# A sandwich layer on one core: the last row's addition on TensorE, the very last row centred ahead of its scale, two blocks re-timed, the FFN's small tensors loaded later

## The chip, the cores and the metric

The kernel runs on 1 core of one Trainium2 chip. The metric is device time in microseconds of one execution; the median of several runs counts. A core has five engines that run their own instruction streams: TensorE (matmuls, into PSUM), VectorE, ScalarE, Pool (GpSimd) and SyncE, which here only issues transfers. They wait for one another by semaphores.

## The reference

The input is 1024 rows of 512 values, in float32. Everything is float32.

```python
x = x + layernorm(attention(layernorm(x)))       # 32 query heads, 8 key/value heads, head size 128, causal
x = x + layernorm(ffn(layernorm(x)))

def attention(x):
    q, k, v = x @ w_q, x @ w_k, x @ w_v          # (512, 4096), (512, 1024), (512, 1024)
    probs = softmax(causal(q k^T * 128 ** -0.5))
    return (probs v) @ w_o                       # (4096, 512)

def ffn(x):
    base_out = x @ base_W.T + base_b             # 512 to 512
    probs = softmax(x @ router_W.T + router_b)   # 15 logits
    w = sum over the 8 largest probs, by expert_map[index]
    h = x @ A.T                                  # 8 experts of rank 16
    return base_out + 2.0 * ((h * w) @ B)

layernorm(x) = (x - mean) / sqrt(var + 1e-5)
```

## The kernel before, in words

**Blocks.** One block is a pair (g, t): a key/value group g of 8 (it has four query heads) and a tile t of 128 rows, of 8. There are 64 blocks. Blocks 0 to 47 (`i < N2`) are groups 0 to 5 in order, each with t = 0 to 7, so that block i is (i//8, i%8); the last 16 interleave groups 6 and 7, two tiles at a time. "Third block" is t=2, "fourth" t=3. Odd groups are g = 1, 3, 5. The rows 512 wide of the eight tiles are gathered in `acc[t]`.

**Inside a block.** The 128 rows are taken in four steps (`NSUB`), each 32 rows of all four heads. `scores(g, t, j)` makes one step's scores on TensorE into a PSUM buffer of two (`s`, two rows of the trace for each 512 columns, since a float32 matmul shows as two). VectorE adds the mask (L691) and takes the maximum (L693), ScalarE the exponential (L698, which frees the PSUM buffer), VectorE the reciprocal (L708), ScalarE the scaling (L709), VectorE a 32x32 transposition into `T` (L715). Pool clears the part of `p` above the diagonal ahead of each step (L672). After the fourth step sixteen transfers bring `T` into `K` (`to_keys`, tile names `K<-T`), on SyncE's queue, or a third of them on Pool's queue in blocks t = 1, 2, 3 of odd groups. Two blocks later `weighted_values` multiplies `K` with the values (`po`, 512 columns, t+1 terms), ScalarE copies the result (L746, `attnT`), and two row tiles at a time `project_o_pair` multiplies with `w_o` (`pa` to `pe`, seven products in 256 columns instead of eight, with sums of operands on VectorE, L796 to L799, and additions into `acc`, L820).

**What fills TensorE.** Between the four score matmuls of block i the main loop hands out other TensorE work, `then`: query, key and value projections for later blocks (`pq`, `pk`, `pv`, also in seven products, in pieces of 128 columns), `po` of block i-2 and, for even i, `pa` to `pe` of the pair before. Each piece has a price in columns, and `run_share` gives step n the pieces whose middle lies between `shares[n]` and `shares[n + 1]` of the total. `weave` merges two lists by price. TensorE keeps the program's order; so do most instructions of the other engines (`keep`, `order`), and the others are placed by a scheduler's estimates.

```python
        if i % 2 and i // 2 + 1 in QW and blocks[i][1] > 1 and 3 < i < N2:
            cut = len(rest) * 3 // 5
            q, rest = weave(q, rest[:cut]), rest[cut:]
```

In an odd-numbered block `rest` is `po`'s terms: two for t=3 (those of block t=1), four for t=5, six for t=7.

**Pool's queue.** Weight and input sums of the seven-product scheme run there (L189: `tx`, `sq`, `sk`, `sv`, `wot`). Right after block 8, (1,0), `prepare_ffn` issues six transfers on Pool's queue for tensors which the FFN needs in the last group (`ra_sb` in two parts, `bt_sb`, `bias_bc`, `rb_bc`, `emap_i`; 256 KB each for three of them). After block 12, (1,4), `prepare_map` builds `mexp` from `emap_i` on VectorE in nine small instructions (L330, L333).

**The end.** When the last score has been taken, an order written out by hand finishes four row tiles c, d, e, f. Row e goes through `ffn_out`: bias (L940), statistics (L344 to L348), reciprocal square root as a power on Pool (L350), shift (L359), normalization on ScalarE (L360), addition into `acc` by VectorE (L944), store. The very last, f, goes through `ffn_out_last`: the same in halves (L976, L977), statistics (L981, L983), power on Pool (L985), then on VectorE centring and scaling in one instruction (L987) and the addition (L988), and its store. The four stores stand in SyncE's queue in the order c, d, e, f. Row e's addition stands in VectorE's queue between f's L983 and L987.

Of the kernel before, what the change touches and what calls it, by code (L numbers as in the profile page):

```python
# [12 lines left out]
ALU = mybir.AluOpType  # L13
# [9 lines left out]
def kernel(  # L23
# [33 lines left out]
    nc = tc.nc  # L57
# [4 lines left out]
    NT = S // P  # L62
# [27 lines left out]
    blocks = [(g, 2 * u + e) for g, u in pairs for e in range(2)]  # L90
    N = len(blocks)
    N2 = (G - 2) * NT
# [5 lines left out]
    def keep(ins):  # L98
        return tc.keep_in_program_order(ins)
# [5 lines left out]
    def matmul(*args, **kw):  # L105
        keep(nc.tensor.matmul(*args, **kw))  # L106
# [181 lines left out]
    ident = const.tile([P, P], F32, tag="ident", name="ident")  # L288
# [77 lines left out]
    def bank(name):  # L366
        return ps_m.tile([P, 512], F32, tag="pm", name=name)
# [271 lines left out]
    def defer(t, *steps, first=False):  # L639

        if held:
            held[t].extend(steps)
            return
        deferred[:0] = steps if first else ()
        deferred.extend(() if first else steps)
# [194 lines left out]
    state = {}  # L840
# [75 lines left out]
    def ffn_out(t):  # L916

        pf = []

        def base(k):  # L920
            if k == 0:

                if t in (c, e):
                    pf.append(ps_s.tile([P, S], F32, tag="s", name=f"pf_{t}")[:, :512])
                else:
                    pf.append(bank(f"pf_{t}"))
            matmul(pf[0], state["hT", t][:, k, :], weights["base", k], start=(k == 0), stop=False)

        def turn_hw():
            pt = bank(f"ptw_{t}")  # L930
            transpose(pt[:, :ER], state.pop(("hw", t)).rearrange("p e r -> p (e r)"), ident)
            hwT = state["hwT", t] = ffn.tile([ER, P], F32, tag="hwT", name=f"hwT_{t}")
            copy = nc.scalar.copy(hwT, pt[:, :P])
            if held:
                keep(copy)

        def finish():
            matmul(pf[0], state.pop(("hwT", t)), bt_sb, start=False, stop=True)
            y = ffn.tile([P, H], F32, tag="hy", name=f"y_{t}", bufs=3)
            order(nc.vector.tensor_tensor(y, pf[0], bias_bc, ALU.add))  # L940
            statistics, norm = layernorm(y, y, f"y{t}", nc.scalar)

            def add_y(by=nc.gpsimd):
                order(by.tensor_tensor(acc[t], y, acc[t], ALU.add))  # L944
                state["done", t] = True

            if held and t == e:
                defer(t, statistics, norm, lambda: add_y(nc.vector))
            else:
                defer(t, statistics, lambda: (norm(), add_y()))  # L950

        w = [(512, lambda k=k: base(k)) for k in range(KC)]
        return w[:2], [(P, turn_hw)], w[2:], [(512, finish)]

    def ffn_out_last(t):


        halves = [slice(n * hn, (n + 1) * hn) for n in range(2)]
        pf = {}

        def base(n, k):
            if k == 0 and n == 0:
                pf[n] = ps_s.tile([P, S], F32, tag="s", name=f"pf_{t}_{n}")[:, :hn]
            elif k == 0:
                pf[n] = bank(f"pf_{t}_{n}")[:, :hn]
            w = weights["base", k][:, halves[n]]
            matmul(pf[n], state["hT", t][:, k, :], w, start=(k == 0), stop=False)

        def finish(*between):

            hwT = state.pop(("hwT", t))
            y = ffn.tile([P, H], F32, tag="hy", name=f"y_{t}", bufs=3)
            stats = small.tile([P, 2, 6], F32, tag="stats2", name=f"stats_y{t}", bufs=1)
            for n in range(2):
                matmul(pf[n], hwT, bt_sb[:, halves[n]], start=False, stop=True)
                keep(nc.vector.tensor_tensor(y[:, halves[n]], pf[n], bias_bc[:, halves[n]], ALU.add))  # L976
                keep(nc.vector.bn_stats(stats[:, n, :], y[:, halves[n]]))  # L977
                if n == 0:
                    between[0]()
            mv = small.tile([P, 2], F32, tag="mv", name=f"mv_y{t}")  # L980
            keep(nc.vector.bn_aggr(mv, stats))  # L981
            ve = small.tile([P, 1], F32, tag="ve", name=f"ve_y{t}")
            keep(nc.vector.tensor_scalar(ve, mv[:, 1:2], EPS, None, ALU.add))  # L983
            rstd = small.tile([P, 1], F32, tag="rstd", name=f"rstd_y{t}")
            keep(nc.gpsimd.tensor_tensor(rstd, ve, neg_half, ALU.pow))  # L985
            between[1]()
            keep(nc.vector.tensor_scalar(y, y, mv[:, 0:1], rstd, ALU.subtract, ALU.mult))  # L987
            keep(nc.vector.tensor_tensor(acc[t], y, acc[t], ALU.add))  # L988
            state["done", t] = True

        return [[(hn, lambda n=n, k=k: base(n, k)) for k in range(KC)] for n in range(2)], finish
# [7 lines left out]
    c, d, e, f = (blocks[k][1] for k in (N - 6, N - 5, N - 2, N - 1))  # L999
# [134 lines left out]
    for i in range(N):  # L1134
        loads(i)
        q, other = projections(i)
        pv = attend(i - 2) if i >= 2 else []
        o, o_pair, ends, begins = [], [], [], []
        for t in complete(i, 3):
            o = project_o(*blocks[i - 3])  # L1140
        if i % 2 == 0 and i >= 4 and blocks[i - 4][0] < G - 1:
            if i == 4:
                rescale_scores()
            o_pair = project_o_pair(*pairs[i // 2 - 2])
        for t in complete(i, 6, 7):
            ends = sum(ffn_out(t), [])
        for t in complete(i, 5):
            begins = ffn_router(t)

        rest = o + weave(o_pair, other + pv[:2] + begins[1:] + pv[2:])  # L1150
        if i in (N2, N2 + NT // 2):
            rest = weave(o_pair, pv) + other
        if i == N2 + 1:
            rest = pv[:3] + other + pv[3:]

        if i % 2 and i // 2 + 1 in QW and blocks[i][1] > 1 and 3 < i < N2:
            cut = len(rest) * 3 // 5
            q, rest = weave(q, rest[:cut]), rest[cut:]
        then = begins[:1] + q + ends[:-1] + rest[:4] + ends[-1:] + rest[4:]
        if i % 2 and i // 2 + 1 in QL:  # L1160
            cut = max(4, len(rest) - 4)
            then = begins[:1] + ends[:-1] + rest[:4] + ends[-1:] + rest[4:cut] + q + rest[cut:]
        shares = [n / NSUB for n in range(NSUB + 1)]
        if o_pair and blocks[i][0] % 2 == 0 and blocks[i][1] == 2 and i < N2:

            shares[3] = 0.8
        for n in range(NSUB):
            scores(*blocks[i], n)
            run_share(then, shares[n], shares[n + 1])
            m = i // 2 + 1  # L1170
            if i % 2 == 0 and m in QL and n == 2:
                todo.extend(last_sums(m))
            if i >= N2 + NT and i // 2 + 1 in QL:
                for dst, p, q, op in [todo.pop(0) for _ in range(min(LATE[i % 2, n], len(todo)))]:
                    keep(nc.gpsimd.tensor_tensor(dst, p, q, op))
            if i % 2 == 0 and m in QW and m not in QL:
                if n == 0 and i < N2:
                    combine_x(pairs[m][1], m)
                if n == (1 if i < N2 else 0):
                    combine_q(m)  # L1180
            g, t = blocks[i]
            if g % 2 and g + 1 < G and n == 1:
                if t == 6:
                    combine_k(g + 1)
                if t == 7:
                    combine_v((g + 1) // GV)
            if (i, n) in ((N2, 3), (N2 + 1, 2), (N2 + 2, 2)):
                combine_x(i - N2 + 1, 0)

            alone = i < 2 or i >= N2 or blocks[i][1] == NT - 1  # L1190
            pool_off(len(pool_jobs) if alone else -(-len(pool_jobs) // (NSUB - n)))
        if i == 2:
            combine_o(0)
        if i == NT:
            prepare_ffn()
        if i == NT + 4:
            prepare_map()
        for t in complete(i, 2):
            reload_x(t)
        ready += complete(i, 7, 8)  # L1200
        for t in [t for t in ready if ("done", t) in state]:
            ready.remove(t)
            ffn_store(t)

        if i >= NT and blocks[i - 2][1] == 0 and blocks[i - 2][0] < G - 1:
            combine_o(blocks[i - 2][0])
            if i >= N2:
                pool_off(len(pool_jobs))
# [79 lines left out]
```

## Time and profile before

| | |
|---|---|
| median of 3 runs | 1056.83 us (1056.42 to 1057.2) |
| profiled execution | 1056.89 us, of which span 1055.1 us |
| TensorE clock granted | 0.998 |
| TensorE busy | 1041.9 us (99%) |
| VectorE, ScalarE, Pool busy | 756.4, 477.0, 286.5 us |
| last TensorE matmul ends, last store is issued | 1046.4, 1050.5 us |

Times in the text are microseconds from the span's start unless they are durations. In the trace's timeline a line has start, duration, engine, line of the kernel, operation, output<-inputs, how many were merged (x4), and in brackets the idle time of the engine ahead of it and what ended it. Matmuls overlap their successors, so their start times tell more than their durations. In the waits a line reads: who, waited for whom: microseconds in total, times, longest. PE is TensorE, DVE VectorE, ACT ScalarE, POOL Pool, SP SyncE; a q behind the name is the engine's sequencer.

### The profile page before, as it was taken

What the parts mean: (1) busy time and instruction counts of PE and PEld (TensorE: products, weight loads), DVE (VectorE), ACT (ScalarE), POOL (GpSimd) and SP (SyncE); (2) the same over time, 40 slices, a digit from 0 to 9 for tenths busy, and PEclk for the clock granted to TensorE, in tenths of its full rate; (3) what the DMA queues carried; (4) which work ended last, traced back from release to release, by engine and by line L of the source; (5) the groups of instructions that cost most, each with busy time, mean ns of one, the idle gap of its engine ahead of it and who ended that gap; (6) DMA issues with size and microseconds to landing.
All of it is one profiled execution on the core that took longest, in us unless ns stands there. A gap on an engine that the chain in (4) does not pass through costs nothing.

```text
span 1055.1 us, 15845 instructions
## 1 busy us (share of the span) xinstructions
PE 1041.9 (99%) x4936; PEld 733.1 (69%) x4936; DVE 756.4 (72%) x1849; ACT 477.0 (45%) x961; POOL 286.5 (27%) x522
## 2 busy tenths in 40 slices
PE   9999999999999999999999999999999999999996
PEld 7766667767787676767787667767788565666553
DVE  4576657876587766887477875886667967687766
ACT  3655434554244544553244543654234654454421
POOL 2513025241030213341031312542162112333112
PEclk9999999999999999999999999999999999999999
DMA  5145352563126352453324443464333673543331
GB/s 189 36 125 137 74 122 70 136 158 83 40 53 163 90 121 68 117 145 81 81 51 120 110 105 72 127 168 120 85 106 91 150 190 90 148 113 95 85 91 40
DMA packets 78515, 112.01 MB, mean 106 GB/s; under 512 B 18176, under 2 KB 49920, under 8 KB 78432
## 3 DMA queue, kind: packets, MB, share of 16 engines
q1 hardware_dynamic: 75248, 106.24, 40.0%
q0 software_dynamic: 2096, 3.46, 1.4%
q10 hardware_dynamic: 1088, 1.31, 0.4%
q8 instruction: 40, 0.66, 0.3%
q14 instruction: 43, 0.35, 0.1%
HBM read 33.34 MB, written 2.10 MB: 34 GB/s over the span
## 4 chain that ended last, share of the span: by engine, by line
PE 91%; DVE 3%; SPq 2%; ACT 1%; DMA 1%; issue 1%; POOL 0%; POOLq 0%; DVEq 0%; ACTq 0%
PE po L106 22%; PE s L106 21%; PE pq L106 18%; PE pv L106 5%; PE pk L106 5%; PE pe L106 4%; PE pa L106 4%; PE pf L106 3%; PE pO L106 2%; PE pc L106 2%; PE pb L106 2%; PE pd L106 2%; SPq L112 2%; DMA K<-T 1%; DVE T L715 1%
## 5 line engine op out<-in xcount | busy, mean ns | idle before, releaser
L709 ACT ACTIVATE p<-p,rec 128x32 f32<-128x32 f32 (+31 forms) x256 | 188.1, 735 | 239.5 <-DVE rec L708 183.9
L106 PE MATMUL po<-K,v 128*128 128x512 f32 x576 | 280.7, 594 | 1.1 <-DMA K<-T 0.8
L106 PE MATMUL s<-kT,qT 128*128 128x512 f32 (+15 forms) x768 | 272.5, 464 | 0.8 <-ACT p L698 0.7
L698 ACT ACTIVATE p<-s,nmax 128x32 f32<-128x32 f32 (+31 forms) x256 | 179.5, 701 | 164.7 <-DVE nmax L693 148.3
L715 DVE STREAM_TRANSPOSE T<-p 128x128 f32<-128x128 f32 (+7 forms) x256 | 197.6, 773 | 52.5 <-ACT p L709 41.0
L106 PEld LDWEIGHTS s<-kT,qT 128*128 128x128 f32 x768 | 140.1, 190 | 116.3 <-issue 103.3
L693 DVE TENSOR_REDUCE nmax<-s 128x1 f32<-128x32 f32 (+31 forms) x256 | 180.1, 704 | 7.2
L672 POOL MEMSET p<- 128x96 f32 (+2 forms) x192 | 29.1, 152 | 544.3 <-DVE T L715 494.7
L106 PEld LDWEIGHTS po<-K,v 128*128 128x128 f32 x576 | 103.1, 190 | 58.8 <-issue 49.5
L513 DVE TENSOR_TENSOR qT<-pq,qT 128x256 f32<-128x256 f32 x174 | 77.8, 461 | 38.0 <-ACT qT L539 20.8
L691 DVE TENSOR_TENSOR s<-s,smask 128x32 f32<-128x32 f32 x256 | 47.9, 187 | 76.4 <-PE s L106 75.5
L106 PEld LDWEIGHTS pq<-xnT,wq 128*128 128x128 f32 x560 | 75.4, 191 | 9.5 <-issue 6.6
L106 PE MATMUL pq<-xnT,wq 128*128 128x128 f32 (+1 forms) x560 | 81.6, 293 | 0.0
L746 ACT COPY attnT<-po 128x512 f32<-128x512 f32 x64 | 37.4, 584 | 71.9 <-PE po L106 71.6
L106 PE MATMUL pa<-wo,attnT 128*128 128x256 f32 x224 | 58.5, 385 | 0.0
L106 PEld LDWEIGHTS pq<-tx,wq 128*128 128x128 f32 x416 | 53.0, 192 | 7.9 <-issue 7.5
L106 PE MATMUL pq<-tx,sq 128*128 128x128 f32 x416 | 57.5, 275 | 0.0
L106 PEld LDWEIGHTS pq<-tx,sq 128*128 128x128 f32 x416 | 53.4, 192 | 5.7 <-issue 5.0
L106 PE MATMUL pq<-tx,wq 128*128 128x128 f32 x416 | 55.4, 275 | 0.0
L106 PEld LDWEIGHTS pa<-wo,attnT 128*128 128x128 f32 x224 | 41.1, 190 | 14.1 <-issue 9.3
L708 DVE RECIPROCAL rec<-total 128x1 f32<-128x1 f32 x256 | 39.2, 153 | 16.2 <-ACT p L698 15.1
L698 ACT ACTIVATION_READ_ACCUMULATOR p<-s,nmax 128x1 f32 x256 | 49.6, 194 | 0.0
(164 smaller groups left out, 1327.9 us busy)
## 6 DMA issues: line engine op xcount, KB each, us to landing
K<-T SPq DMA_DIRECT2D x128, 128.0 KB, 2.4
K<-T SPq DMA_DIRECT2D x128, 112.0 KB, 2.3
wq<-in_w_q_dram SPq DMA_DIRECT2D x27, 512.0 KB, 5.1
K<-T SPq DMA_DIRECT2D x128, 96.0 KB, 2.2
K<-T SPq DMA_DIRECT2D x128, 80.0 KB, 2.1
wo<-in_w_o_dram SPq DMA_DIRECT2D x32, 256.0 KB, 3.5
K<-T SPq DMA_DIRECT2D x108, 64.0 KB, 2.0
K<-T SPq DMA_DIRECT2D x113, 48.0 KB, 1.9
```

The costliest lines, as they stand in the source:

```text
L106: keep(nc.tensor.matmul(*args, **kw))
L112: keep(by.dma_start(dst, src))
L513: nc.vector.tensor_tensor(dst, src, to, ALU.add)
L672: keep(nc.gpsimd.memset(p[:, t * P + (j + 1) * SQ : (t + 1) * P], 0.0))
L691: keep(nc.vector.tensor_tensor(s[:, n - SQ : n], s[:, n - SQ : n], smask, ALU.add))
L693: keep(nc.vector.tensor_reduce(nmax, s[:, :n], AX.X, ALU.max, negate=True))
L698: keep(nc.scalar.activation(p[:, :n], s[:, :n], AF.Exp, bias=nmax, accum_out=total))
L708: keep(nc.vector.reciprocal(rec, total))
L709: keep(nc.scalar.mul(p[:, :n], p[:, :n], rec))
L715: nc.vector.transpose(turned[g, t][:, :, j, :, :].rearrange("p b k q -> p k b q"), p[:, :full].rearrange("p (k b q) -> p k b q", b=R, q=SQ),)
L746: copy = nc.scalar.copy(o, po)
```

## The change

- Row e's last addition: instead of VectorE adding, TensorE multiplies `acc[e]` and then y by the identity into one PSUM bank, and ScalarE copies the bank into `acc[e]`.
- Row f: VectorE first subtracts the mean (one instruction that needs no power), then multiplies with the power and adds in one instruction.
- t=3 of groups 1 to 5: of `po`'s two terms none is woven into the query pieces (before: one); for t=5 and 7 as before.
- t=2 of odd groups: the fourth score matmul comes after 0.8 of the other work instead of 0.75, as it did already in even groups.
- `prepare_ffn` after block 12 instead of 8, `prepare_map` after block 16 instead of 12.

```diff
+            def add_on_pe():
+                pm = bank(f"padd_{t}")
+                matmul(pm, ident, acc[t], start=True, stop=False)
+                matmul(pm, ident, y, start=False, stop=True)
+                keep(nc.scalar.copy(acc[t], pm))
+                state["done", t] = True
+
             if held and t == e:
-                defer(t, statistics, norm, lambda: add_y(nc.vector))
+                defer(t, statistics, norm, add_on_pe)
...
-            keep(nc.vector.tensor_scalar(y, y, mv[:, 0:1], rstd, ALU.subtract, ALU.mult))
-            keep(nc.vector.tensor_tensor(acc[t], y, acc[t], ALU.add))
+            keep(nc.vector.tensor_scalar(y, y, mv[:, 0:1], None, ALU.subtract))
+            keep(nc.vector.scalar_tensor_tensor(acc[t], y, rstd, acc[t], ALU.mult, ALU.add))
...
-            cut = len(rest) * 3 // 5
+            cut = len(rest) * (4 if blocks[i][1] == 3 else 6) // 10
...
-        if o_pair and blocks[i][0] % 2 == 0 and blocks[i][1] == 2 and i < N2:
+        if o_pair and blocks[i][1] == 2 and i < N2:
             shares[3] = 0.8
...
-        if i == NT:
+        if i == NT + 4:
             prepare_ffn()
-        if i == NT + 4:
+        if i == NT + 8:
             prepare_map()
```

## The prediction, before the change was run

> **What bounds the kernel now.** I read the page first: TensorE is busy nearly all the time and carries the chain.
>
> ```profile
> PE 1041.9 (99%) x4936; PEld 733.1 (69%) x4936; DVE 756.4 (72%) x1849; ACT 477.0 (45%) x961; POOL 286.5 (27%) x522
> PE 91%; DVE 3%; SPq 2%; ACT 1%; DMA 1%; issue 1%; POOL 0%; POOLq 0%; DVEq 0%; ACTq 0%
> ```
>
> So an edit pays only where it closes a hole in TensorE's row or shortens the end after its last matmul. The page's matmul ends are modelled, so I measured holes by start times. Two 256-column rows start 0.216 us apart (eight in 1.73 us), two of 224 columns 0.189 apart; a start later than that is a hole. The waits of TensorE name the two that this diff can reach:
>
> ```profile
> PE po L106 <- DMA K<-T: 0.8, 1, 0.8
> PE s L106 <- ACT p L698: 0.7, 2, 0.3
> ```
>
> The first, in TensorE's timeline, and on the chain that ended last:
>
> ```profile
> 148.88 0.54 PE L106 MATMUL s<-kT,qT 128*128 128x224 f32 x2
> 150.19 2.38 PE L106 MATMUL po<-K,v 128*128 128x512 f32 x5 [0.76 <-DMA K<-T]
> ...
> 141.82 6.69 DMA K<-T
> 148.53 1.61 DMA K<-T
> ```
>
> `po` of block (0,7) was due at 148.88+2x0.189=149.26 and began at 150.19: 0.93 late. It waited for a transfer that took 6.69 us. The DMA view of 134 to 152 us shows what it met, and the page shows its usual time, 2.4:
>
> ```profile
> K<-T SPq DMA_DIRECT2D x16, 128.0 KB, 3.0
> ra_sb<-in_a_t_dram POOLq DMA_DIRECT2D x1, 256.0 KB, 5.0
> bt_sb<-in_b_t_dram POOLq DMA_DIRECT2D x1, 256.0 KB, 5.5
> bias_bc<-in_base_b_dram POOLq DMA_DIRECT2D x1, 256.0 KB, 6.6
> ...
> K<-T SPq DMA_DIRECT2D x128, 128.0 KB, 2.4
> ```
>
> The second, in group 3's third block (TensorE, then ScalarE), with the same place in group 2, where the share is 0.8 already:
>
> ```profile
> 411.19 1.03 PE L106 MATMUL pd<-wo,sums 128*128 128x256 f32 x4
> 412.55 0.91 PE L106 MATMUL s<-kT,qT 128*128 128x384 f32 x2 [0.33 <-ACT p L698]
> 412.29 0.20 ACT L698 ACTIVATION_READ_ACCUMULATOR p<-s,nmax 128x1 f32 x1
> ...
> 289.46 0.59 PE L106 MATMUL pe<-wo,sums 128*128 128x256 f32 x2
> 289.95 0.91 PE L106 MATMUL s<-kT,qT 128*128 128x384 f32 x2
> ```
>
> Due at 411.19+0.86=412.05, it began at 412.55, when ScalarE had freed the score buffer. In group 2 two rows of `pe` fill that time and the start is 0.06 late.
>
> Last, the end:
>
> ```profile
> 1048.07 0.68 DVE L944 TENSOR_TENSOR acc<-y,acc 128x512 f32<-128x512 f32 x1
> 1048.30 0.86 POOL L985 TENSOR_TENSOR rstd_y<-ve_y,neg_half 128x1 f32<-128x1 f32 x1 [1.69 <-DVE ve_y L983]
> 1049.19 0.55 DVE L987 TENSOR_SCALAR y<-y,mv_y,rstd_y 128x512 f32<-128x512 f32 x1 [0.44 <-POOL rstd_y L985]
> 1049.77 0.69 DVE L988 TENSOR_TENSOR acc<-y,acc 128x512 f32<-128x512 f32 x1
> L1284 POOLq DRAIN  x3: 46/102/5961, 1048.3 to 1054.7; - x3
> ```
>
> The last store is issued at 1050.50 and lands at 1052.50; SyncE has checked its semaphores by 1053.07. But Pool's own drain, queued behind the power, runs 5.96 us from 1048.27 to 1054.23, and the closing barrier comes after it. Stores have 1.16 us to spare.
>
> **FFN's small tensors later.** `prepare_ffn` issues six Pool DMAs (139.10 to 142.79, 3.69 us of Pool); they go from behind block 8 to behind block 12, Pool's `tx` sums there ending at 192.69, so about 192.7 to 196.4. Without them the sixteen K transfers of block 7, the last issued at 143.89, land in about 2.4 us, near 146.3, three before `po` is due. The hole goes: 0.93, and 0.07 by which the first row after it ran slow. **-1.00 us.** At the new place: block 11's K transfers end at 194.19, 2.7 before their reader; on Pool the six pass only `p`'s memset of 194.25, now about 196.4, whose exponential begins at 201.43; `wo` (four of 256 KB, issued 192.87 to 194.84) isn't read before its sums on Pool at 294.1. Then come block 12's K transfers, issued from 197.78, landed 210.21, read at 210.92: 0.71 us of cover, the thinnest. I take nothing there, because they ask for 80 KB each 0.63 us against block 7's 128 KB, and the DMA share was 0.56 (192 to 211) against 0.82 (134 to 150); the other end is a rival. `prepare_map` goes from block 12 to block 16: 0.17+0.70 us of VectorE leave the spot just before the transpose that releases block 12's K (so it may start up to 0.87 sooner) and come behind an addition that ends at 261.92 after 1.63 us of idleness; cover: TensorE has projections there. Nothing.
>
> **Share 0.8 in odd groups' third block.** Two rows of `pe` (0.43 us) move in front of the fourth scores. In groups 3 and 5 (holes at 411.8 and 656.3, both 0.50 and 0.10 of slow restart) the hole becomes group 2's 0.06 and 0.10: 2x0.43, **-0.86 us.** Group 1 has no hole at 166.93; its scores come 0.43 later, against 3.0 us of cover of that block's K. In groups 3 and 5 the scores keep their absolute time while TensorE's later work comes 0.43 sooner, and VectorE may put `acc<-pe` (0.69) before their maximum, so the block's K loses 0.4 to 1.1 us of cover: 2.4 in group 3, 1.0 in group 5. Zero to 0.1.
>
> **Fourth block.** The diff says odd groups, but the condition holds for t=3 of groups 1 to 5. The first of two `po` terms moves behind the query pieces. Four pieces of 128 columns stand for one of 512, so each score matmul keeps its distance in TensorE's work; the last `po` stays where it was, and VectorE's sums wait for that one. No hole over 0.07 us lies in these blocks. Nothing; bounds 0.4 either way, a hole of the size seen elsewhere (0.44 at 326.4).
>
> **The end.** Row e: its addition leaves VectorE (0.68 us). The first 512-column pair runs in TensorE's idleness after 1046.4; the second waits for ScalarE's y (done 1047.84) and ends at 1047.90+0.43+0.59=1048.92; the copy, priced by L380's 0.59, ends near 1049.6. So row e's store goes from 1048.78 to about 1049.64 and holds SyncE until 1050.0. Row f: centring (0.55 by L987) starts at 1048.07 and ends at 1048.62. It isn't free beside the power: Pool's power takes 0.55 where VectorE reads PSUM (1029.46), but here it ended 0.41 behind L944's end. Centring being 0.13 shorter than L944, the power ends near 1049.03. The fused multiply-add has no row; 0.55 (one input) to 1.38 (two passes of L988) bound it, and I take L988's 0.69 for its two tensor inputs: 1049.76, store at 1050.02 behind row e's. If the drain counts from the power's end, as I take it, the span ends **0.13 us** sooner; if it counts from its own start, nothing. If instead stores set the end, row f's packets queue behind row e's (0.8 us each, by packets of the last two): 1049.64+2.0+0.8=1052.4, 0.06 sooner; without that queueing 0.47. The Trainium skill, "SBUF — State Buffer", section "SBUF: two separate sides", says that the port pair shared by VectorE and GpSimd is an exclusive lock, and that the blocked side starts about 0.115 us after VectorE's end. By it the title's "while Pool takes its power" is no overlap; the rows agree (0.86 against 0.55). With a true overlap the power would end at 1048.85 and the sum would be 0.18 better.
>
> **Sum:** 1.00+0.86+0.13=1.99. The profiled execution took 1056.89 (span 1055.1 and 1.8 around it), against a median of 1056.83: 1054.90 from the one, 1054.84 from the other. **Forecast 1054.8 us.** What a measurement of this kernel can tell from no change is about 0.2%, 2.1 us, so the forecast lies on that line.
>
> **Rivals.** *More than summed:* the hole at 326.4 (0.44, K of group 2's fourth block, landing 3.57 us after its issue) closes with the re-timed block, and the end gains 0.47 because stores bind: 1.00+0.86+0.44+0.47=2.77, 1054.1. For it: Pool's other two drains took 0.10 and 0.05, so the long one may wait for something outside Pool; against: nothing in the t=3 edit moves that block's last transpose. The Trainium skill, "VectorE: DVE Perf Modes", section "The DRAIN you can't avoid", gives boilerplate drains about 12 ns, by which the stores would bind; the 5961 ns above speaks against it here.
>
> *The re-timing is handed back:* group 5's third block runs out of its 1.0 us, or group 3's scores wait for the later exponential in block four (I count 0.4 us of cover). Then 0.86 returns: 1055.7. Against it: even groups live with 0.8, though their fourth block is longer.
>
> *The collision moves (slower):* the six loads meet `wo` and block 12's K. Block 7's last transfer landed in 6.1 us; at that price instead of 2.1, less 0.71, TensorE waits 3.3 us at 210.9: 1056.83-1.99+3.3=1058.1. It decides for slower when that landing takes over 2.1+0.71+1.99=4.8 us. Against: spare DMA time before the last is issued at 208.09.
>
> **Chances.** Forecast 0.62 (own range 1054.1 to 1055.4; about 0.34 of it beyond 0.2%), more 0.18, handed back 0.10, collision 0.10 (half of it over 0.2%). Faster 0.34+0.18=0.52; same 0.28+0.10+0.05=0.43; slower 0.05. The range 1053.8 to 1056.2 holds the first three and leaves out the collision and the outer edges.
>
> **What would show it.** Right: no TensorE wait on `K<-T` near 149, no 0.33 us waits on `p` L698, K transfers near 141 landing in 2.4 us, block 12's `po` unbroken near 209, power 0.7 to 0.8 us. Wrong: a new TensorE wait on `K<-T` near 210 or in group 5's fifth block, waits on `p` in a fourth block, or an end more than 0.3 us off its old distance from the last `pf` matmul.

## The result

The changed kernel took 1054.93 us (median of 21 runs, 1054.42 to 1055.62) against 1056.77 for the kernel before beside it (21 runs, 1055.92 to 1057.3): ratio 0.9983, 95% interval 0.9976 to 0.9989. That is 1.84 us less. The profiled execution took 1054.94 with a span of 1053.2, clock 0.999. The forecast was 1054.8.

The page after, and TensorE's longest waits:

```profile
PE 1043.6 (99%) x4940; PEld 733.7 (70%) x4940; DVE 755.5 (72%) x1848; ACT 477.1 (45%) x962; POOL 285.8 (27%) x522
```
```profile
PE idle L109 <- POOL ident masks.py:199: 1.5, 1, 1.5
PE padd L106 <- ACT y L360: 0.7, 1, 0.7
PE pc L106 <- DVE acc L818: 0.7, 1, 0.7
PE po L106 <- DMA K<-T: 0.3, 1, 0.3
```

The two waits of before are gone from this list (`s` for `p` L698) or another one (the `po` that still waits for `K<-T` is at 995.3, not at 149). TensorE's timeline at the two places:

```profile
148.99 0.54 PE L106 MATMUL s<-kT,qT 128*128 128x224 f32 x2
149.37 1.88 PE L106 MATMUL po<-K,v 128*128 128x512 f32 x4
...
410.72 0.59 PE L106 MATMUL pe<-wo,sums 128*128 128x256 f32 x2
411.22 0.91 PE L106 MATMUL s<-kT,qT 128*128 128x384 f32 x2
```

`po` follows the scores at their 2x0.189 us, and two rows of `pe` stand where the 0.50 us of waiting stood. The DMA view of 134 to 152 us has the sixteen K transfers with nothing beside them:

```profile
K<-T SPq DMA_DIRECT2D x16, 128.0 KB, 2.4
K<-T SPq DMA_DIRECT2D x11, 16.0 KB, 1.9
```

The end, from the timeline and from the rows of the closing barrier (its line is L1293 now):

```profile
1046.42 0.48 DVE L996 TENSOR_SCALAR y<-y,mv_y 128x512 f32<-128x512 f32 x1
1046.65 0.65 POOL L993 TENSOR_TENSOR rstd_y<-ve_y,neg_half 128x1 f32<-128x1 f32 x1 [1.69 <-DVE ve_y L991]
1047.34 0.75 DVE L997 SCALAR_TENSOR_TENSOR acc<-y,rstd_y,acc 128x512 f32<-128x512 f32 x1 [0.44 <-POOL rstd_y L993]
1047.40 0.59 ACT L952 COPY acc<-padd 128x512 f32<-128x512 f32 x1 [1.22 <-PE padd L106]
```
```profile
L1293 POOLq DRAIN  x3: 46/102/5751, 1046.6 to 1052.9; - x3
L1293 SPq DRAIN  x3: 7/7/7, 1051.2 to 1052.6; - x3
```

Pool's long drain shrank from 5961 to 5751 ns, as the power in front of it shrank from 0.86 to 0.65 us.

The following table gives TensorE's holes (late start and slow restart together, us) at the places that matter, for the traces of the experiments too. The last row is from the first `pv` matmul to the last group of `pf`, which leaves out the first 8 us and the end.

| near us | before | before again | FFN alone | share alone | cut alone | end alone | share + cut | after | after, no cut |
|---|---|---|---|---|---|---|---|---|---|
| 55 | 0.38 | 0.16 | 0.28 | 0.08 | 0.08 | 0.42 | 0.16 | 0.44 | 0.08 |
| 149 | 1.00 | 1.36 | 0 | 0.84 | 0.94 | 0.91 | 0.83 | 0 | 0 |
| 326 | 0.44 | 0 | 0.42 | 0 | 0 | 0 | 0 | 0 | 0 |
| 412 | 0.60 | 0.60 | 0.60 | 0.17 | 0.60 | 0.60 | 0.17 | 0.17 | 0.17 |
| 424 | 0 | 0 | 0 | 0.64 | 0 | 0 | 0 | 0 | 0.64 |
| 656 | 0.60 | 0.60 | 0.60 | 0.17 | 0.60 | 0.60 | 0.17 | 0.17 | 0.17 |
| 670 | 0 | 0 | 0 | 0.64 | 0 | 0 | 0 | 0 | 0.64 |
| 698 | 0 | 0 | 0 | 0 | 0 | 0 | 0.08 | 0.20 | 0 |
| 995 | 0.16 | 0.15 | 0.15 | 0.46 | 0.15 | 1.23 | 0.31 | 0.50 | 0.45 |
| 1011 | 0.84 | 0.87 | 0.86 | 0.51 | 0.86 | 0.29 | 1.06 | 0.85 | 0.51 |
| first `pv` to last `pf` | 1037.27 | 1036.90 | 1036.15 | 1036.77 | 1036.42 | 1037.22 | 1036.05 | 1035.56 | 1035.86 |

Between the first traces of before and after, four holes close by 1.00+0.44+0.43+0.43=2.30 and others open by 0.34+0.20+0.06=0.60 (near 995, 698 and 55). The row of distances gives 1.71. The hole near 995 is 0.31 to 0.66 in all eight traces of kernels with the share and 0.14 to 0.16 in five of the six without it (the sixth, 1.23, is told further down), so some 0.3 us of it goes with the share; why stays open.

### The profile page after: what moved, and what is told of

It reads as the page before. It is cut to its first block, busy times and chain, and to the rows that moved or that the text cites. A ratio compares the mean times of both kernels' runs of the same rounds, so it can differ in the third digit from the quotient of the medians.

```text
span 1053.2 us, 15841 instructions
## 1 busy us (share of the span) xinstructions
PE 1043.6 (99%) x4940; PEld 733.7 (70%) x4940; DVE 755.5 (72%) x1848; ACT 477.1 (45%) x962; POOL 285.8 (27%) x522
## 3 DMA queue, kind: packets, MB, share of 16 engines
q10 hardware_dynamic: 1088, 1.31, 0.4%
## 4 chain that ended last, share of the span: by engine, by line
PE 94%; DVE 3%; SPq 1%; issue 1%; ACT 1%; POOL 0%; DMA 0%; POOLq 0%; DVEq 0%; ACTq 0%
PE po L106 22%; PE s L106 21%; PE pq L106 19%; PE pv L106 5%; PE pk L106 5%; PE pe L106 5%; PE pa L106 4%; PE pf L106 3%; PE pO L106 2%; PE pc L106 2%; PE pd L106 2%; PE pb L106 2%; SPq L112 1%; PE pl L106 1%; PE idle L109 1%
## 5 line engine op out<-in xcount | busy, mean ns | idle before, releaser
L698 ACT ACTIVATE p<-s,nmax 128x32 f32<-128x32 f32 (+31 forms) x256 | 179.5, 701 | 161.1 <-DVE nmax L693 141.8
L513 DVE TENSOR_TENSOR qT<-pq,qT 128x256 f32<-128x256 f32 x174 | 77.4, 459 | 35.7 <-ACT qT L539 19.1
L698 ACT ACTIVATION_READ_ACCUMULATOR p<-s,nmax 128x1 f32 x256 | 49.6, 194 | 0.0
```

Of the source, the lines that this page charges most:

```text
L513: nc.vector.tensor_tensor(dst, src, to, ALU.add)
L698: keep(nc.scalar.activation(p[:, :n], s[:, :n], AF.Exp, bias=nmax, accum_out=total))
```

## The experiments

**The four parts, each alone on the kernel before.** Medians of 11 executions each, against 1056.62. None of the four intervals excludes 1, so what a part does is read from its trace and not from its time.

*FFN's small tensors:*

```diff
-        if i == NT:
+        if i == NT + 4:
             prepare_ffn()
-        if i == NT + 4:
+        if i == NT + 8:
             prepare_map()
```

> Only the FFN's small tensors are moved (the six Pool DMAs four blocks later, and the expert map's two VectorE steps four blocks later). My theory: the hole before block (0,7)'s po goes (0.92 + 0.08 us in the trace of before), and nothing takes its place, so the last group of pf matmuls starts 1.0 us sooner and the time is 1055.8 against 1056.8 of before. Rival 'collision moves': block 12's po waits for K and the gain is below 0.5. Second question: the hole of 0.44 us at 326.4, gone in the changed kernel, for which nothing in my steps accounts. If it goes here too, more is gained, 1.4 us (1055.4), and it belongs neither to the share nor to the fourth blocks.

1055.76 us, ratio 0.9993 (0.9984 to 1.0001): 0.86 less. The hole at 149 is gone, block 7's K last landed at 146.30, and block 12's K landed 1.14 us ahead of its reader, so no collision. The hole at 326 is here (0.42), so this edit does not close it.

*The share:*

```diff
-        if o_pair and blocks[i][0] % 2 == 0 and blocks[i][1] == 2 and i < N2:
+        if o_pair and blocks[i][1] == 2 and i < N2:
             shares[3] = 0.8
```

> Only the share of 0.8 for the third blocks of odd groups. My theory: the holes at 411.8 and 656.3 shrink from 0.50 to 0.07 us each, 0.86 in all: 1055.9 us against 1056.8, with the hole near 149 unchanged. Rival 'handed back': a new wait of TensorE in the fourth or fifth block of group 3 or 5 takes some of it, and the gain is under 0.5. If the hole that the changed kernel has at 697.8 (0.20 us, group 5's fifth block) is here too, it is the price of this edit; if not, it has another cause.

1056.83 us, ratio 1.0002 (0.9993 to 1.0011): no gain. The holes at 412 and 656 shrink by 0.43 each, as forecast; two new ones of 0.64 stand at 424 and 670. (The texts on record give the second as 0.56: there another hole of 0.08, which stands beside it in every kernel, was taken off.) TensorE's waits of this kernel name them, and the timelines of VectorE and TensorE show why:

```profile
PE s L106 <- DVE qT L513: 0.8, 2, 0.4
```
```profile
423.20 0.20 DVE L691 TENSOR_TENSOR s<-s,smask 128x32 f32<-128x32 f32 x1 [0.26 <-PE s L106]
423.77 0.71 DVE L715 STREAM_TRANSPOSE T<-p 128x512 f32<-128x512 f32 x1 [0.38 <-ACT p L709]
424.41 0.65 DVE L693 TENSOR_REDUCE nmax<-s 128x1 f32<-128x512 f32 x1
424.98 0.74 DVE L513 TENSOR_TENSOR qT<-pq,qT 128x256 f32<-128x256 f32 x2
```
```profile
423.22 1.06 PE L106 MATMUL pq<-tx,sq 128*128 128x128 f32 x8
424.11 1.02 PE L106 MATMUL po<-K,v 128*128 128x512 f32 x2
425.54 1.24 PE L106 MATMUL s<-kT,qT 128*128 128x512 f32 x4 [0.40 <-DVE qT L513]
```

The next scores need queries that L513 adds up from pieces of `pq`; the first of the two L513 at 424.98 makes the last of them. On VectorE it stands behind a transposition that itself waits for ScalarE, and behind the maximum. In the kernel before, VectorE and TensorE at the same place:

```profile
424.33 0.20 DVE L691 TENSOR_TENSOR s<-s,smask 128x32 f32<-128x32 f32 x1 [0.53 <-PE s L106]
424.55 0.42 DVE L513 TENSOR_TENSOR qT<-pq,qT 128x256 f32<-128x256 f32 x1
424.89 0.68 DVE L693 TENSOR_REDUCE nmax<-s 128x1 f32<-128x512 f32 x1
425.49 0.70 DVE L715 STREAM_TRANSPOSE T<-p 128x512 f32<-128x512 f32 x1
```
```profile
424.35 1.06 PE L106 MATMUL pq<-tx,sq 128*128 128x128 f32 x8
425.24 1.02 PE L106 MATMUL po<-K,v 128*128 128x512 f32 x2
426.10 1.16 PE L106 MATMUL s<-kT,qT 128*128 128x512 f32 x4
```

TensorE's program in the fourth block is the same in both kernels: one `po` (0.86 us) stands between the pieces and the scores, and the eight pieces begin 1.75 us before the scores are due. But before, that L513 stood ahead of the maximum and the transposition and ended 1.13 us before the scores began. The share's edit touches only TensorE's program, in the third blocks; VectorE's order changed with it, since L513 is one of the instructions that the scheduler's estimates place. So the hole comes of VectorE's new order. The 0.43 us by which TensorE is ahead would by these rows have left some 0.7 of the 1.13 as cover, an estimate; no kernel had the share with VectorE's old order, so this is read from the rows and not tested.

*The fourth blocks' cut:*

```diff
-            cut = len(rest) * 3 // 5
+            cut = len(rest) * (4 if blocks[i][1] == 3 else 6) // 10
```

> Only the cut in the fourth blocks, one po behind the query pieces. My theory: nothing, within 0.1 us of before in the place of the last pf matmuls, no hole comes or goes. Rival 'more than summed': the hole of 0.44 us at 326.4, in the block after a re-timed one, closes here, and the time is 0.4 us shorter. Where neither this kernel nor the ones with another part alone close it as a part of their work, but it comes and goes with the place of some other transfer, it is the third case: chance of the transfers' meeting.

1056.63 us, ratio 1.0002 (0.9993 to 1.0011). No hole comes or goes through it. The one at 326 is absent here, but also in the share alone and in the end alone, which has the program of before up to its last 10 us.

*The end:* `add_on_pe` for row e, and

```diff
-            keep(nc.vector.tensor_scalar(y, y, mv[:, 0:1], rstd, ALU.subtract, ALU.mult))
-            keep(nc.vector.tensor_tensor(acc[t], y, acc[t], ALU.add))
+            keep(nc.vector.tensor_scalar(y, y, mv[:, 0:1], None, ALU.subtract))
+            keep(nc.vector.scalar_tensor_tensor(acc[t], y, rstd, acc[t], ALU.mult, ALU.add))
```

> Only the two edits of the tail. Everything up to the last pf matmuls stays within 0.1 us of before. My theory (Pool's drain sets the end and counts from the end of its last instruction, the power): the power ends 0.2 us sooner after the last pf matmul than before, Pool's drain ends 5.07 us after it as in both traces, and the span is 0.2 us shorter, 1056.6. Rival (the stores set the end): SyncE's last check moves by less than that and the span follows it. With 0.2 us alone the comparison of times cannot tell this from no change; the distances in the trace can.

1056.5 us, ratio 0.9997 (0.9988 to 1.0006). From the start of the last `pf` group the power ends after 3.65 us (before: 3.86), Pool's drain 5.07 later, and the span after 9.51 (before: 9.82; after: 9.51). So 0.21 comes from the power, and 0.1 from a SyncE drain of 130 ns within the closing barrier, which this kernel and after do not have (it is 115 or 130 ns in every kernel without this edit and 7 in every kernel with it; why stays open). In the closing barrier of before it is the longest of three:

```profile
L1284 SPq DRAIN  x3: 7/7/130, 1053.0 to 1054.8; - x3
```

**Share and cut together**, on the kernel before, 11 executions, against 1056.77.

> The share of 0.8 and the cut in the fourth blocks together, nothing else changed from before. In the traces of each alone, the share closed the holes at 411.8 and 656.3 (0.86 in all) but two new ones of 0.64 and 0.56 stand at 424.5 and 671.5, in the fourth blocks of groups 3 and 5, where the scores wait for qT of VectorE L513; the cut alone did nothing. New theory: the cut is the share's other half, because its po between the last query piece and the scores covers that wait. Then both new holes are gone here and the holes at 411.8 and 656.3 are 0.17 each: 0.86 less than before, 1055.8 us. Rival (the two edits are independent, as my prediction had it): the new holes stay, and the sum is that of the two alone, 1056.7 to 1056.9.

1055.98 us, ratio 0.9993 (0.9984 to 1.0002): 0.79 less. Both new holes are gone. TensorE's timeline of this kernel shows two `po` (four rows) between the pieces and the scores, and VectorE's shows L513:

```profile
423.06 0.38 PE L106 MATMUL pq<-tx,sq 128*128 128x128 f32 x2
423.28 1.88 PE L106 MATMUL po<-K,v 128*128 128x512 f32 x4
425.00 1.16 PE L106 MATMUL s<-kT,qT 128*128 128x512 f32 x4
```
```profile
421.98 0.72 DVE L513 TENSOR_TENSOR qT<-pq,qT 128x256 f32<-128x256 f32 x2
```

The transposition and the maximum still stand ahead of the last L513 here, but the scores no longer need that one: with a `po` moved behind them the pieces come sooner, and the sum that the scores need is the first of these two, which ended at 422.36, 2.64 us before them.

**After without the cut**, 11 executions, against 1056.49.

> After with the fourth blocks' cut put back to what it was, all else as in after. If the cut is the share's other half, the two holes of 0.64 and 0.56 stand near 423 and 670 again, where the scores wait for qT, and the time is 1.2 us over after's 1054.9, 1056.1. If the cut does nothing, as my prediction had it, the time is after's, 1054.9, and no hole over 0.17 us stands in the fourth blocks of groups 3 and 5.

1055.58 us, ratio 0.9993 (0.9984 to 1.0002). Both holes of 0.64 are back, at `qT` and with VectorE in the order of the share alone, so the cut is what closes them. The time is only 0.65 over after's, half of what was expected: in this trace the holes near 55, 698 and 1011 are 0.36, 0.20 and 0.34 shorter. The one near 1011 is 0.51 in both kernels that have the share without the cut, so part of this may be given back by the program; that wasn't separated from chance.

**What sets the end.** Two in-place multiplications by 1.0 behind row f's fused addition, one execution:

```diff
             keep(nc.vector.scalar_tensor_tensor(acc[t], y, rstd, acc[t], ALU.mult, ALU.add))
+            for _ in range(2):
+                keep(nc.vector.tensor_scalar(acc[t], acc[t], 1.0, None, ALU.mult))
```

> After, with two in-place multiplications by 1.0 of row f's sum (some 0.5 us each on VectorE, as the centring took 0.48) ahead of its store, so that the last store is issued about 1.0 us later; Pool's program is that of after. If Pool's drain sets the end: SyncE's last check moves from 1051.3 to 1052.3, still no later than the drain's end at 5.07 us behind the power, and the span does not move, 1053.2 give or take what other holes do. If the stores set the end, the distance from the last pf matmul to the end of the span grows by 1.0 us.

The last store was issued 0.58 us later (the two took 0.43 each) and SyncE's last check moved from 1051.29 to 1051.60, less than expected, as a store that is no longer right behind row e's lands in 2.01 instead of 2.27. The span didn't follow: 9.50 us from the last `pf` group, against 9.51. The stores do not set the end.

A memset as the last instruction of Pool, one execution:

```diff
             keep(nc.gpsimd.tensor_tensor(rstd, ve, neg_half, ALU.pow))
+            spare = small.tile([P, 1], F32, tag="rstd", name=f"spare_y{t}")
+            keep(nc.gpsimd.memset(spare, 0.0))
```

> After, with one more instruction at the very end of Pool's program: a memset of one column behind row f's power. It is to tell what the 5.07 us of Pool's drain count from. If from Pool's last instruction, whatever it is: the drain ends 5.07 us after the memset's end, 0.1 to 0.3 us later than in after relative to the last pf matmuls. If the 5.07 us belong to the power, its tail runs in parallel: the drain ends 5.07 us after the power as before. If a cheap last instruction has a short drain of its own: the drain ends well before, and the stores set the end, 1.0 us sooner.

The power ended at 1046.89, the memset at 1046.94, the drain at 1052.01: 5.07 us behind the memset, and 5.12 behind the power. In before and after the distance from the power was 5.07, so the drain counts from Pool's last instruction of whatever kind. The two readings lie only 0.05 us apart here; the next kernel is the stronger test.

Row f's power off Pool, six executions, against 1056.77:

```diff
+            first = small.tile([P, 1], F32, tag="rstd", name=f"first_y{t}")
+            keep(nc.scalar.activation(first, ident[:, 0:1], AF.Sqrt))
...
-            rstd = small.tile([P, 1], F32, tag="rstd", name=f"rstd_y{t}")
-            keep(nc.gpsimd.tensor_tensor(rstd, ve, neg_half, ALU.pow))
+            root = small.tile([P, 1], F32, tag="rstd", name=f"root_y{t}")
+            keep(nc.scalar.activation(root, ve, AF.Sqrt))
             between[1]()
             keep(nc.vector.tensor_scalar(y, y, mv[:, 0:1], None, ALU.subtract))
+            rstd = small.tile([P, 1], F32, tag="rstd", name=f"rstd_y{t}")
+            keep(nc.vector.reciprocal(rstd, root))
```

> After, with row f's power taken off Pool: ScalarE's square root and VectorE's reciprocal behind the centring give the same number, and a first square root on one column, ahead of row e's norm, brings ScalarE's table load forward. Pool's last instruction is then row e's power, which ended at 1044.96 in the trace of after. My theory (the end is Pool's drain, 5.07 us behind Pool's last instruction): the drain ends near 1050.0, and now the last store sets the end; SyncE's last check was at 1051.29, the closing 0.8 us behind it: span 1052.1 against 1053.2, and 1.0 to 1.1 us less than after's time, about 1053.9. Rival (the stores set the end already, or the drain waits for something outside Pool): the drain still ends near 1052.4 and the time stays that of after, 1054.9, within 0.2.

1053.15 us, ratio 0.9968 (0.9956 to 0.9980) to before, where after has 0.9983 (0.9976 to 0.9989). Its timelines of ScalarE and Pool, and Pool's row of the closing barrier:

```profile
1043.92 1.28 ACT L980 ACT_TABLE_LOAD   x1
1045.22 0.20 ACT L980 ACTIVATE first_y<-ident 128x1 f32<-128x1 f32 x1
1045.92 0.81 ACT L360 ACTIVATE y<-y,shift_y,rstd_y 128x512 f32<-128x512 f32 x1 [0.50 <-DVE shift_y L359]
1047.14 0.20 ACT L995 ACTIVATE root_y<-ve_y 128x1 f32<-128x1 f32 x1 [0.41 <-DVE ve_y L993]
```
```profile
1045.01 0.55 POOL L350 TENSOR_TENSOR rstd_y<-ve_y,neg_half 128x1 f32<-128x1 f32 x1 [1.13 <-DVE ve_y L348]
```
```profile
L1297 POOLq DRAIN  x3: 46/102/5647, 1045.0 to 1052.3; - x3
```

Row e's power is now Pool's last instruction. It ended at 1045.56, and the drain at 1050.63, 5.07 behind it. SyncE's last check at 1051.83 is later, so the stores set the end, 8.34 us behind the last `pf` group: 1.17 less than after, where 1.0 to 1.1 was expected. The 1.78 between the medians holds 0.6 more. The profiled execution was the longest of the six, 1054.37, and only 0.57 shorter than that of after, so I put the difference down to the holes that differ from run to run; this isn't shown.

The same with the stores in the order f, e, six executions, against 1056.45:

```diff
-    for t in (c, d, e, f):
+    for t in (c, d, f, e):
         ffn_store(t)
```

> The kernel with row f's square root on ScalarE, with the last two stores in the other order, f and then e. In its trace the last store now sets the end: row f's sum was ready at 1048.36, but its store was issued at 1048.98 behind row e's of 1048.56, and landed in 2.27 us where the one before it took 2.02. With the order turned f's goes at about 1048.41 and e's at about 1048.83, 0.15 sooner than the last one now; if the later landing is the second store's price it lands at 1051.1 in place of 1051.25: the distance from the last pf matmuls to the end 0.15 us shorter, and the time 1053.0. If the second store isn't delayed behind the other way round, 0.4. Rival (Pool's drain still sets the end): the drain ended at 1050.63, 1.2 before SyncE's last check, so that it can't.

1053.26 us, ratio 0.9969 (0.9957 to 0.9981). The distance is 8.17 us, 0.17 shorter; the time does not tell the two apart.

**The holes that come and go.** The kernel before once more, one execution:

> The kernel before once more, unchanged, for a second trace of one program. In the traces so far the hole at 326.4 (0.44 us; K of group 2's fourth block landing 3.6 us after its issue in place of 2.0) stands in two kernels of six and the one near 997 is 0.15 to 1.23 us, in kernels that are the same program up to there; where a hole is long, a 16 KB read on the queue that brings TensorE's instructions took 1.0 to 1.5 us beside the last K transfers. If this is chance of a run: the holes at 55, 326 and 997 come out otherwise here than in the first trace of before, by 0.1 to 1 us, with the reads at other times by up to some us; those at 149, 411.8 and 656.3 are as before within 0.16 us. If they belong to the program, all are as in the first trace.

1056.55 us, and the table's third column: 326 goes from 0.44 to 0, 55 from 0.38 to 0.16, while 412 and 656 stay within 0.002. The hole at 149, too, varies with the run by more than expected (1.36).

In fourteen traces the read on the instruction queue comes 1.30 to 1.32 us after the issue of block 19's last K transfer in two (before, and the FFN edit alone), and that transfer lands after 3.57 and 3.63 us. In the twelve others the read comes 1.60 us or more after it, and the transfer lands after 2.0 to 2.1. In the kernel with the end alone, the read fell at 989.6 among block 61's K transfers; one issue then held SyncE for 1.67 us in place of 0.59, and the hole near 995 was 1.23. The DMA view of 989.1 to 990.5 us there:

```profile
q8 instruction: 1, 0.02, 6.8%
issues: line engine op xcount, KB each, median us to landing
K<-T SPq DMA_DIRECT2D x3, 64.0 KB, 3.2
```

In before that read came at 996.5, behind the transfers, and the DMA view of 989 to 992 us has the same transfers at 2.0:

```profile
q14 instruction: 1, 0.01, 0.6%
issues: line engine op xcount, KB each, median us to landing
K<-T SPq DMA_DIRECT2D x5, 64.0 KB, 2.0
```

To move the reads on purpose, 18 idle transposes in place of 26, one execution:

```diff
-    for n in range(26):
+    for n in range(18):
         transpose(idle[:, ts(n % KC, P)], ident, ident)
```

> Before, with 18 idle transposes at the start in place of 26, so that all of TensorE's program lies 8 transposes (16 instructions with their weight loads) further ahead in memory, and nothing else is changed. If the reads on TensorE's instruction queue come at fixed places of the program, each comes later by the time of eight matmuls, 1.7 to 3.4 us: the one of 324.3 near 326 to 328, so that the last K transfers of group 2's fourth block land in 2.0 us, the hole at 326.4 isn't there, and other transfers, those issued some 1.3 us ahead of the read's new place, take 3 us and more. If the reads come by time or by chance of up to some us, no such shift is seen over the forty reads.

1056.74 us. Inconclusive: against the first trace of before the forty reads moved by anything from 2.4 us earlier to 11 later, and the one in question by 0.4. The hole at 326 was absent, but so it is in most traces. That the reads delay the transfers rests on these times alone; no kernel here moved them at will.

## Why the prediction was right, and where it was not

**FFN's tensors (-1.00).** Right. K's last landing was put near 146.3 and came at 146.26. Block 12's cover, put at 0.71 with nothing taken from it, was 0.60 in after. The collision with `wo` did not delay that K: landed at 209.43 against 210.03 due.

**The share (-0.86) and the fourth block (0).** The sizes of the two holes were right, 0.43 each, and the sum of both edits nearly so (0.79 measured, with an interval that just includes no change), but the split was wrong. The step that failed is the share's "Zero to 0.1": alone, the share costs 2x0.64 us in the fourth blocks. The prediction asked there for the cover of K and for one change of VectorE's order in the third block, `acc<-pe` ahead of the maximum. That change came (the addition starts at 414.1 in the share alone and at 415.8 in before), but the order changed in the fourth block as well, and there it delays L513, a producer of the scores that the prediction did not ask about. "Nothing" is right for the cut alone; on top of the share, the cut closes those 2x0.64. That both errors cancel is luck: the forecast holds because the change has both edits. The rival "handed back" is what the share alone does, though at `qT` and not at K or the exponential that it named.

**The end (-0.13).** Mechanism right: the drain counts from the power's end. The size was 0.21, since centring took 0.48 and not L987's 0.55, and SyncE's drain gave another 0.1 that no step had. The multiply-add took 0.75 (0.69 assumed, bounds 0.55 to 1.38). Row f's store went out 1.94 us after `ve` (1.87 forecast). Behind centring the power ended at 1047.30, 0.40 after VectorE's end at 1046.90, where it was 0.41 before: the trace agrees with the rule of the Trainium skill, "SBUF — State Buffer", section "SBUF: two separate sides", in that the centring delays the power. It does not show that the two never overlap: row e's power took 0.55, and one that began only after VectorE's end would at that length have ended later than 0.40 behind it.

**"More than summed".** The hole at 326.4 did close, but no edit closes it; it stands in two of fourteen traces. By its own trace after gained 0.44 there and lost 0.60 elsewhere (0.34 of it near 995, the hole that goes with the share), so the total (1.95 between the two profiled executions, 1.84 between the medians) came out near the sum of 1.99.

**The rival of the short drain.** The prediction weighed a rule of the Trainium skill, "VectorE: DVE Perf Modes", section "The DRAIN you can't avoid": boilerplate drains of about 12 ns. In the closing barrier of before, VectorE, ScalarE and TensorE drain twice: their first drains end 0.03 to 0.05 us behind the engine's last instruction, and their second last 19, 14 and 13 ns, near that figure. Pool's first does not agree: it ended 5.07 us behind Pool's last instruction, and it set the end of before and of after. These drains carry a line of the kernel's own file (L1284 in before), so whether they are the ones that the rule means is not shown.

**What can be told.** The prediction took 0.2%, 2.1 us, as the least difference that can be told from none. With 21 executions of each kernel the interval is 0.11 to 0.24% below no change, so the 1.84 us are clear of it.

## What to carry to other kernels

When work is moved on one engine, list every producer that the next steps wait for, operand by operand, and look for each one's place in its engine's queue, after the edit as well as before it: where a scheduler places instructions, an edit of TensorE's order can turn VectorE's. An edit that is worth nothing alone can be the cover that another edit needs, so try the two together and apart. When the end of a kernel is studied, look at which engine's drain ends last: finishing Pool's program 2.3 us sooner (1.31 us behind the last `pf` group instead of 3.65) took 1.17 us off here, more than the change to the last rows' arithmetic did (0.31). And compare two traces of the same program before a hole is credited to an edit: here 0.4 to 1.1 us of holes come and go by themselves.

## What the runs showed of the hardware that I had not expected

- Pool's first closing drain ended 5.07 us after its last instruction in every kernel, fourteen traces in all, be that the power (1049.16 to 1054.23 in before), row e's power with 2.8 us of VectorE's work still to come (1045.56 to 1050.63), or a memset (1046.94 to 1052.01).
- The page's instruction queues read 40 packets of 16 KB (q8) in each execution, 0.9 to 1.7 us each near the places above. The K transfers of 64 KB that had one beside them early on their way took 3.1 to 3.7 us to land in place of 2.0, and one issue on SyncE's queue 1.67 in place of 0.59. That q8 is TensorE's I take from its instructions being the most (4940 matmuls and as many loads).
- Those reads do not come at fixed times of one program: two executions of before had one at 184.6 and 182.1, another at 996.5 and 997.5, and a kernel equal to them up to there at 989.6.
